# Self-attention of a decoder layer: where v's store to DRAM stands in the queue, and which queues begin v's four copies

## The chip, the cores and the metric

The kernel runs on one core of a Trainium2 chip. The metric is the device time of one launch in microseconds (us), as the median of three runs. Everything is 32-bit floating point. Besides the timed runs there is one execution recorded by the hardware profiler; its page and trace are what the text reads from.

## The reference

A decoder layer works on x of shape (2, 1024, 256): self-attention, cross-attention to a context of 77 rows, and a feed-forward part that only half of the tokens pass through, each followed by an addition and a layer norm. The change touches the self-attention only:

```python
q, k, v = split_heads(x @ Wq), split_heads(x @ Wk), split_heads(x @ Wv)   # 16 heads of 64
q, k = apply_rope(q), apply_rope(k)
sim = where(causal, einsum('bid,bjd->bij', q, k) * 64 ** -0.5, -inf)
out = einsum('bij,bjd->bid', softmax(sim, axis=-1), v)
x = layernorm(x + merge_heads(out) @ Wo + bo)
```

## The kernel before

**Pairs.** Two heads make a pair of 128 columns. There are 2 x 8 = 16 pairs, numbered 0 to 15, and an object `Pair` has one method for each step. Tokens are cut in eight tiles of 128. The steps have short names in lists of text: a number in front of a name is the pair's, and in the list `steps` the number beside a name says which pair is meant, relative to the period: `("w", 1)` in period 5 is for pair 6, `("V7", -1)` for pair 4. So three pairs are in work at once: in one period the outputs of pair n-1, the scores of pair n and the projections of pairs n+1 and n+2. The first two pairs follow a list of their own (`opening`), the last ones another (`ending`). The order of the instructions on each engine, and of the DMAs on each queue, is the order of these lists; each engine and each queue takes its own in that order, and an instruction that waits holds all behind it.

**The steps that matter here**, with their lines:

- `P` and `E`: projections on TensorE (L268 for q and k, L303 for v) and their evacuation by ScalarE (L276 into `raw`, L312 into `v`). `Ek1` fills the second half of `raw`, `Ev4` and `Ev0` fill the two halves of `v`. The tile `v` has one buffer: pair n+2's `Ev0` may write it only after pair n+1's `v` has been stored.
- `d0`, `d1` (`swap`, L219): two DMAs each, from SBUF to SBUF, that swap neighbouring partitions of `raw` into `turned`, for tokens 0 to 511 and for tokens 512 to 1023. `c`, `s`, `a`: GpSimd's multiplications by cosine (L288), by sine (L291) and the addition (L295) that make the rotated k and q.
- `S0` to `S4`: scores on TensorE (L342). `S0` needs only the first half of the rotated k and q, `S1` is the first that needs the second half.
- `T`, `X`, `R`: masked minimum on VectorE (L355), exponentials on ScalarE (L363), transposes on VectorE (L372).
- `w` (`spread`, through `begin`, L219): one DMA on SP's queue that stores `v`, 512 KB, into a DRAM tile `v_d`.
- `l` (`copies`, L322): four DMAs that load `v_d` into `v4` four times, each into other 32 partitions, 512 KB each. They stand on the queue of ScalarE, which begins them between its own instructions. The tile `v4` has one buffer, so they wait for the outputs of the pair before.
- `V0` to `V7` (`output`, L410): the products of the probabilities with `v4`, 488 small matmuls a pair, 64 columns by 32 rows, with a weight load for each. `S0` stands before `V0`, `S1` between `V1` and `V2`, `S2` between `V4` and `V5`, `S3` behind `V7`.
- `O`: evacuation of the outputs (L422). `D` and `B` (L219): the inverse sums go to DRAM (`inv_d`) and come back spread over 128 partitions (`over`). `M` multiplies on GpSimd, `W` stores the pair's output.

**The gate.** `begin` puts a DMA on SP's queue. The last matmul of `V1` is left in the list `gate`; the next DMA that goes through `begin` takes it out and waits for that matmul. In the list `steps` the next one is `d0` of pair n+1, and so `d0`, `B`'s two DMAs and `w`'s one follow one another on SP's queue once `V1` is done.

Of the kernel before, what the change touches and what calls it, by code (L numbers as in the profile page):

```python
# [17 lines left out]
B, T, C = 2, 1024, 256  # L18
# [4 lines left out]
NT = T // P  # L23
# [11 lines left out]
def decoder_layer(  # L35
# [23 lines left out]
    nc = tc.nc  # L59
# [80 lines left out]
    keys = [(b, hp) for b in range(B) for hp in range(NP)]  # L140
# [5 lines left out]
    with (  # L146
# [99 lines left out]
        class Pair:  # L246
# [71 lines left out]
            def copies(self):  # L318

                self.v4 = s1.tile([P, K4, P], F32, tag="v4", name="v4")  # L320
                for r in range(4):
                    nc.scalar.dma_start(  # L322
                        self.v4[r * R32 : (r + 1) * R32, :, :].rearrange("k (c n) d -> k c (n d)", c=4),
                        self.v_d.rearrange("c k e -> k c e"),
                    )
# [73 lines left out]
            def output(self, n):  # L399
                if n == 0:  # L400
                    self.po = [ring.tile([P, NT, R32], F32, tag="t", name="po_self") for _ in range(4)]
                for k in range(4):
                    for j in range(2):
                        first = (NT * n + n, NT * (n + 1) + n)[j]
                        step = (1, NT)[j]
                        last = first + (NT - 1 - n) * step + 1

                        for r in range(k if n == NT - 1 else 0, 4):
                            rows = slice(r * R32, (r + 1) * R32)
                            ins = TE.matmul(  # L410
                                self.po[r][j * D : (j + 1) * D, n:, :],
                                self.v4[rows, NT * k + n, j * D : (j + 1) * D],
                                p_t[rows, first:last:step, k * R32 : (k + 1) * R32],
                                start=(n == 0 and k == 0), stop=(n == NT - 1 and k == r),
                            )
                if n == 1 and self.n < len(keys) - 1:
                    gate[:] = [ins]

            def gathered(self, r):
# [18 lines left out]
        class Closing:  # L438
# [47 lines left out]

        steps = [
# [40 lines left out]
            0Ev4 0T01 1Pq1 0X00 0c1 0s1 0X01 1Eq1 1Ek1 1Pv0 0a1 0S1 2L 0R00 0w 0R01 1d1 1Pv4 1c1 1Pq0 0T10 0T11  # L528
            0S2 1Ev4 0T21 0X10 1Ev0 1Eq0 1Pk0 1s1 1w 0X11 2Pq1 0T20 0l 0R10 1Ek0 1d0 0S3 0R11 0X21 0X20 0T30
            2Pk0 1a1 0T31 0X30 1c0 0S4 0X31 0R20 1s0 0R30 0R21 1a0 2Eq1 0T40 3L 2Pv4 0T41 2Pv0 0X40 0X41 2Ek0  # L530
            0R31 0R40 2Pq0 2Ev4 5= 1S0 0R41 1T00 2Eq0 2Ev0 0V0 1T01 0V1 2w 0V2 1S1 1T11 0V3 1X00 2d0 0V4 0V5 1T10
            1S2 1X01 1X11 1R00 0V6 0V7 1X10 0O0 1T20 1T21 1S3 1R10 1R01 0O1 2c0 1l 1X20 1T31 2Pk1 0O3 1T30 0O2
            3Pv4 0Q 2Ek1 1S4 2c1 1X30 2s0 1X21 3Pq1 1R20 3Ev4 3Pv0 2a0 1R11 3Pk0 0I 1T41 2d1 1R30 1X31 3Pq0 1T40
            2S0 1R21 1X41 1X40 1R31 1R40 0D 1R41 2T00 3Ek0 2s1 3Eq1 4L 2a1 3Eq0 3Ev0 1V0 1V1 0B 2T01 2X00 1V2 2S1
            1V3 1V4 2T10 2T11 1V5 2R00 2S2 2X01 2T20 2T21 1V6 2X11 2R01 1V7 3d0 3c0
        """


        ending = """
            14S3 14R11 15s0 14X20 12M 14R20 14X10 14X21 14R10 13O0 14l 13O1 14R21 14T31 15Pk1 15a0 13Q 14T30 13I  # L540
            14S4 14X31 14X30 13O2 14R31 14T41 14X41 14T40 14R30 14R41 4C 12W 13D 15Ek1 15d1 5A 15c1 4Y 13O3 14X40 14R40
            15S0 15s1 15T01 15a1 14V0 15T00 15X01 14V1 13B 14V2 15S1 14V3 14V4 15T10 15T11 15X00 14V5
            15R00 15X11 15S2 14V6 14V7 15X10 15T20 15T21 14O0 15R01 15S3 14O3 5C 15R10 15l 15X21 13M 15T30 15X20
# [602 lines left out]
```

## Time and profile before

| | us |
|---|---|
| median of 3 runs | 831.27 (830.59 to 837.27) |
| profiled execution, its own time | 842.25 |
| its span | 840.5 |
| TensorE busy in the span | 796.4 (95%) |
| VectorE, ScalarE, GpSimd busy | 581.4, 356.6, 367.6 |
| outputs (L410), first to last matmul | 57.3 to 553.6 |

A time of the profiled execution is counted from the start of its span; 1.75 us of its own time lie outside. It took 11 us more than the median of the timed runs. "x" in front of a number counts instructions. A time in square brackets in the timeline is how long the engine stood idle before the row, and what ended the wait; "issue" stands for idle time in which the engine waited for nothing that the profile shows. The mean granted TensorE clock was 0.985 of the full one. Queue q1 holds the DMAs that SP began, q10 those of ScalarE, and q8 brings TensorE's instructions: 90 packets, 1.47 MB, so 16 KB each.

### The profile page before, as it was taken

The numbers are of one execution on the slowest core, as the hardware profiler recorded it, in microseconds if no ns is written. First come the engines' busy times: TensorE is split into PE (matmuls) and PEld (weight loads), VectorE is DVE, ScalarE is ACT, GpSimd is POOL, SyncE is SP. The second block draws the span as 40 slices with busy tenths as digits, with TensorE's granted clock in tenths as the row PEclk, the third lists the DMA queues.
The fourth block names the chain that finished last, engine by engine and source line by source line (L and its number), as shares of the span: only waits on it lengthen the run. The fifth ranks groups of instructions, "written<-read, shape, count | busy, mean of one in ns | idle before, by whom it ended". The sixth has DMA issues, their size and how long they took to land.

```text
span 840.5 us, 26580 instructions
## 1 busy us (share of the span) xinstructions
PE 796.4 (95%) x11432; PEld 629.2 (75%) x11432; DVE 581.4 (69%) x1345; ACT 356.6 (42%) x842; POOL 367.6 (44%) x261
## 2 busy tenths in 40 slices
PE   8999999999999899999999989899999999998996
PEld 4566688888788787788787867589778888876655
DVE  2558679668668568668776796535477788876673
ACT  2545455556456455554544554200443332333220
POOL 2733554555454554463661653213032222261574
PEclk9999999999999999999999999899999999999999
DMA  5445387577468467567474585564360000011131
GB/s 176 140 135 138 117 216 181 180 197 195 128 168 205 149 187 184 172 170 183 161 195 130 150 208 161 130 188 151 132 210 1 1 1 0 1 51 51 51 101 50
DMA packets 65328, 112.32 MB, mean 134 GB/s; under 512 B 6497, under 2 KB 43707, under 8 KB 65211
## 3 DMA queue, kind: packets, MB, share of 16 engines
q1 hardware_dynamic: 54459, 72.87, 26.9%
q10 hardware_dynamic: 9216, 33.56, 18.6%
q0 software_dynamic: 1536, 4.20, 1.3%
q8 instruction: 90, 1.47, 0.8%
q14 instruction: 27, 0.22, 0.1%
HBM read 71.24 MB, written 22.59 MB: 112 GB/s over the span
## 4 chain that ended last, share of the span: by engine, by line
PE 79%; DVE 10%; issue 4%; POOL 4%; DMA 1%; ACT 1%; POOLq 0%; SPq 0%; DVEq 0%; ACTq 0%
PE po_self L410 17%; PE ps_scores L342 16%; PE pp_kq L268 13%; PE pp_v L303 7%; PE po_proj L473 5%; PE ps_cross L945 5%; PE po_cross L997 4%; DVE reach L800 2%; PE pp_h L888 2%; PE po_ffn L899 2%; DVE pT L372 2%; PE unread L244 1%; PE pt_p L977 1%; POOL e L966 1%; POOL comp L830 1%
## 5 line engine op out<-in xcount | busy, mean ns | idle before, releaser
L355 DVE CUSTOM_DVE_ANT_0 p<-ps_scores,fence 128x512 f32<-128x512 f32 (+7 forms) x256 | 179.7, 751 | 127.2 <-PE ps_scores L342 126.8
L363 ACT ACTIVATE p<-p,neg 128x768 f32<-128x768 f32 (+7 forms) x256 | 196.3, 768 | 162.5 <-DVE neg L355 160.6
L410 PE MATMUL po_self<-pT,v 32*64 32x256 f32 (+6 forms) x7808 | 160.4, 298 | 22.3 <-issue 17.5
L372 DVE STREAM_TRANSPOSE pT<-p 128x768 f32<-128x768 f32 (+7 forms) x256 | 175.8, 740 | 3.4 <-ACT p L363 1.8
L410 PEld LDWEIGHTS po_self<-pT,v 32*64 32x64 f32 x7808 | 139.1, 133 | 47.6 <-issue 36.3
L342 PE MATMUL ps_scores<-kq 64*128 64x256 f32 (+3 forms) x1056 | 151.8, 420 | 2.9 <-issue 1.3
L342 PEld LDWEIGHTS ps_scores<-kq 64*128 64x128 f32 x1056 | 95.0, 191 | 45.2 <-issue 29.8
L291 POOL TENSOR_TENSOR turned<-turned,sin 128x1024 f32<-128x1024 f32 x31 | 73.1, 2360 | 109.7 <-DMA turned<-raw 105.0
L268 PE MATMUL pp_kq<-xT,w_pair 128*128 128x256 f32 (+2 forms) x516 | 118.8, 382 | 1.3 <-ACT xT L203 0.8
L288 POOL TENSOR_TENSOR kq<-raw,cos 128x1024 f32<-128x1024 f32 x31 | 73.3, 2363 | 103.8 <-ACT raw L276 103.8
L268 PEld LDWEIGHTS pp_kq<-xT,w_pair 128*128 128x128 f32 x516 | 87.1, 191 | 25.2 <-issue 11.3
L966 POOL TENSOR_TENSOR e<-e,inv 128x616 f32<-128x616 f32 x32 | 38.2, 1215 | 113.8 <-DVE inv L965 96.1
L120 POOL TENSOR_TENSOR rs<-ve,neg_half 128x1 f32<-128x1 f32 x48 | 27.6, 577 | 113.3 <-DVE ve L118 112.1
L295 POOL TENSOR_TENSOR kq<-kq,turned 128x1024 f32<-128x1024 f32 x31 | 73.4, 2369 | 1.4
L997 PE MATMUL po_cross<-packed,pT 128*128 128x256 f32 (+1 forms) x320 | 72.5, 381 | 0.0
L945 PE MATMUL ps_cross<-wqk,x1T 128*128 128x308 f32 x256 | 69.2, 423 | 0.0
L997 PEld LDWEIGHTS po_cross<-packed,pT 128*128 128x128 f32 (+1 forms) x320 | 60.7, 192 | 8.9
L303 PEld LDWEIGHTS pp_v<-w_pair,xT 128*128 128x128 f32 x512 | 61.1, 192 | 4.0 <-issue 2.2
L303 PE MATMUL pp_v<-w_pair,xT 128*128 128x128 f32 x512 | 62.2, 275 | 0.0
L945 PEld LDWEIGHTS ps_cross<-wqk,x1T 128*128 128x128 f32 x256 | 47.4, 190 | 16.2 <-issue 0.7
L958 ACT ACTIVATE e<-e 128x616 f32<-128x616 f32 x32 | 22.9, 717 | 83.0 <-DVE e L954 83.0
L473 PE MATMUL po_proj<-wo,attnT 128*128 128x256 f32 x224 | 51.6, 381 | 1.5 <-ACT out_pair L422 1.0
(128 smaller groups left out, 830.7 us busy)
## 6 DMA issues: line engine op xcount, KB each, us to landing
v<-v_d ACTq DMA_DIRECT2D x64, 512.0 KB, 8.4
turned<-raw SPq DMA_DIRECT2D x64, 256.0 KB, 4.5
v_d<-v SPq DMA_DIRECT2D x16, 512.0 KB, 4.6
over<-inv_d SPq DMA_DIRECT2D x32, 256.0 KB, 4.7
attn_d<-out_pair SPq DMA_DIRECT2D x14, 512.0 KB, 3.8
attnT<-attn_d SPq DMA_DIRECT2D x8, 512.0 KB, 5.4
vo_d<-vo SPq DMA_DIRECT2D x2, 1232.0 KB
attnT<-attn_d SPq DMA_DIRECT2D x3, 768.0 KB, 6.5
```

The source lines that it names most:

```text
L268: TE.matmul(pp[:, cols], self.w[:, c, "kq".index(of), :], x_ts[self.b, n][:, c, cols], start=(c == 0), stop=(c == NC - 1),)
L288: E.tensor_tensor(self.kq[:, :, n * NB : (n + 1) * NB], self.raw[n], self.twice(cos, n), ALU.mult)
L295: E.tensor_tensor(dst, dst, self.turned[n], ALU.add)
L303: TE.matmul(pv[:, i, :], x_ts[self.b, 2 * n // NT][:, c, toks], self.w[:, c, 2, :], start=(c == 0), stop=(c == NC - 1),)
L342: TE.matmul(self.ps[j][:, cols], self.kq[rows, 1, t * P : (t + 1) * P], self.kq[rows, 0, cols.start - at : cols.stop - at], start=True, st ...
L355: V.tensor_tensor_reduce(p[:, span], self.ps[j][:, span], fence[:, T - (t + 1) * P :], -SCALE, -MASKED, ALU.add, ALU.min, neg[:, i : i + 1],)
L363: A.activation(p[:, span], p[:, span], AF.Exp, bias=neg[:, i : i + 1], scale=-1.0, accum_out=self.sums[:, j, t : t + 1],)
L372: V.transpose(p_t[:, first : first + t * step + 1 : step, :], self.p[g, j][:, span].rearrange("p (n k) -> p n k", k=P),)
L410: ins = TE.matmul(self.po[r][j * D : (j + 1) * D, n:, :], self.v4[rows, NT * k + n, j * D : (j + 1) * D], p_t[rows, first:last:step, k * R ...
L473: TE.matmul(self.po, of, wo[:, c, :], start=(c == 0), stop=(c == NP - 1))
L945: TE.matmul(ps[:, g, : Q * S], self.x_t[:, c, :], wqk[:, c, self.b, h : h + Q, :].rearrange("p h s -> p (h s)"), start=(c == 0), stop=(c = ...
L997: TE.matmul(po, self.p_t[:w, k, :], packed[self.b][:w, k, :], start=(k == 0), stop=(k == NK - 1))
```

## The change

There are three edits:

1. `w` moves from behind `V1` (after `d0` and `B`) to behind `V7` of the same period, and the last matmul of `V7` is left in `gate` too, so that the store waits for it. In the ending, `15w` is put at the front for the same reason. SP's order in a period was: `d0` (2 DMAs), `B` (2), `w` (1), `d1` (2), and so on. It becomes: `d0` (2), `B` (2), `w` (1, now waiting for `V7`), two of `l`'s copies, `d1` (2), and so on.
2. In the opening, `2d0` moves ahead, so that it and not `2w` is what takes `V1`'s gate, and `3d0` moves ahead of `0B` for the same reason.
3. Of `l`'s four copies the first and third stay on ScalarE's queue, and the second and fourth go to SP's.

The instructions of TensorE, VectorE and GpSimd are the same and in the same order, and so are the computing ones of ScalarE.

```diff
                 for r in range(4):
-                    nc.scalar.dma_start(
+                    (nc.scalar, nc.sync)[r % 2].dma_start(
                         self.v4[r * R32 : (r + 1) * R32, :, :].rearrange("k (c n) d -> k c (n d)", c=4),
                         self.v_d.rearrange("c k e -> k c e"),
                     )
...
-                if n == 1 and self.n < len(keys) - 1:
+                if n in (1, NT - 1) and self.n < len(keys) - 1:
                     gate[:] = [ins]
...
-            ("T00", 0), ("T01", 0), ("s1", 0), ("V0", -1), ("a1", 0), ("V1", -1), ("d0", 1), ("B", -2), ("w", 1), ("S1", 0), ("V2", -1),
+            ("T00", 0), ("T01", 0), ("s1", 0), ("V0", -1), ("a1", 0), ("V1", -1), ("d0", 1), ("B", -2), ("S1", 0), ("V2", -1),
...
-            ("V6", -1), ("T21", 0), ("V7", -1), ("X10", 0), ("X20", 0), ("O1", -1), ("S3", 0),
+            ("V6", -1), ("T21", 0), ("V7", -1), ("w", 1), ("X10", 0), ("X20", 0), ("O1", -1), ("S3", 0),
...
-            ... 0V0 1T01 0V1 2w 0V2 1S1 1T11 0V3 1X00 2d0 0V4 0V5 1T10
-            1S2 1X01 1X11 1R00 0V6 0V7 1X10 ...
+            ... 0V0 1T01 0V1 2d0 0V2 1S1 1T11 0V3 1X00 0V4 0V5 1T10
+            1S2 1X01 1X11 1R00 0V6 0V7 2w 1X10 ...
...
-            ... 1V0 1V1 0B 2T01 2X00 1V2 2S1
-            1V3 1V4 ... 1V7 3d0 3c0
+            ... 1V0 1V1 3d0 0B 2T01 2X00 1V2 2S1
+            1V3 1V4 ... 1V7 3c0
...
-            14S3 14R11 15s0 ...
+            15w 14S3 14R11 15s0 ...
```

More of the change, by code (lines that the diff above doesn't have):

```diff
@@ L530, in decoder_layer @@
             2Pk0 1a1 0T31 0X30 1c0 0S4 0X31 0R20 1s0 0R30 0R21 1a0 2Eq1 0T40 3L 2Pv4 0T41 2Pv0 0X40 0X41 2Ek0
-            0R31 0R40 2Pq0 2Ev4 5= 1S0 0R41 1T00 2Eq0 2Ev0 0V0 1T01 0V1 2w 0V2 1S1 1T11 0V3 1X00 2d0 0V4 0V5 1T10
-            1S2 1X01 1X11 1R00 0V6 0V7 1X10 0O0 1T20 1T21 1S3 1R10 1R01 0O1 2c0 1l 1X20 1T31 2Pk1 0O3 1T30 0O2
+            0R31 0R40 2Pq0 2Ev4 5= 1S0 0R41 1T00 2Eq0 2Ev0 0V0 1T01 0V1 2d0 0V2 1S1 1T11 0V3 1X00 0V4 0V5 1T10
+            1S2 1X01 1X11 1R00 0V6 0V7 2w 1X10 0O0 1T20 1T21 1S3 1R10 1R01 0O1 2c0 1l 1X20 1T31 2Pk1 0O3 1T30 0O2
             3Pv4 0Q 2Ek1 1S4 2c1 1X30 2s0 1X21 3Pq1 1R20 3Ev4 3Pv0 2a0 1R11 3Pk0 0I 1T41 2d1 1R30 1X31 3Pq0 1T40
-            2S0 1R21 1X41 1X40 1R31 1R40 0D 1R41 2T00 3Ek0 2s1 3Eq1 4L 2a1 3Eq0 3Ev0 1V0 1V1 0B 2T01 2X00 1V2 2S1
-            1V3 1V4 2T10 2T11 1V5 2R00 2S2 2X01 2T20 2T21 1V6 2X11 2R01 1V7 3d0 3c0
+            2S0 1R21 1X41 1X40 1R31 1R40 0D 1R41 2T00 3Ek0 2s1 3Eq1 4L 2a1 3Eq0 3Ev0 1V0 1V1 3d0 0B 2T01 2X00 1V2 2S1
+            1V3 1V4 2T10 2T11 1V5 2R00 2S2 2X01 2T20 2T21 1V6 2X11 2R01 1V7 3c0
         """
         ending = """
-            14S3 14R11 15s0 14X20 12M 14R20 14X10 14X21 14R10 13O0 14l 13O1 14R21 14T31 15Pk1 15a0 13Q 14T30 13I
+            15w 14S3 14R11 15s0 14X20 12M 14R20 14X10 14X21 14R10 13O0 14l 13O1 14R21 14T31 15Pk1 15a0 13Q 14T30 13I
             14S4 14X31 14X30 13O2 14R31 14T41 14X41 14T40 14R30 14R41 4C 12W 13D 15Ek1 15d1 5A 15c1 4Y 13O3 14X40 14R40
```

## The prediction

> **What bounds the kernel now.** I read the page first, then the list of waits, and then the timeline of TensorE and of the DMA queues around one pair.
>
> ```profile
> PE 796.4 (95%) x11432; PEld 629.2 (75%) x11432; DVE 581.4 (69%) x1345; ACT 356.6 (42%) x842; POOL 367.6 (44%) x261
> ...
> q8 instruction: 90, 1.47, 0.8%
> ...
> PE po_self L410 <- issue: 17.5, 16, 2.4
> ```
>
> TensorE is busy for 95% of the span, so while the pairs run only what it waits for can be won. The third row (waits: us in total, times, longest) says what that is in the output products: 17.5 us in 16 stalls in which nothing visible is missing. The second row gives a suspect, TensorE's own instructions: 90 packets of 16 KB. An output matmul with its weight load takes 2 of 256 places in such a packet and 18 ns or so (3.5 us for 128), so in `V2` to `V7` TensorE eats one packet in 2.4 us.
>
> The timeline of TensorE and SP for one pair (start, us, row):
>
> ```profile
> 280.18 3.86 PE L410 MATMUL po_self<-pT,v 32*64 32x192 f32 x192
> 283.96 1.56 PE L342 MATMUL ps_scores<-kq 64*128 64x512 f32 x8
> 285.45 1.05 PE L410 MATMUL po_self<-pT,v 32*64 32x96 f32 x65
> 288.86 1.43 PE L410 MATMUL po_self<-pT,v 32*64 32x64 f32 x103 [2.36 <-issue]
> ...
> 278.53 1.11 SPq L219 DMA_DIRECT2D turned<-raw  x2
> 279.69 2.87 SPq L219 DMA_DIRECT2D over<-inv_d  x2
> 282.65 0.54 SPq L219 DMA_DIRECT2D v_d<-v  x1
> ```
>
> and the queues in the stretch from 286.2 to 288 (packets, MB, share):
>
> ```profile
> q1 hardware_dynamic: 18, 0.04, 5.3%
> q8 instruction: 1, 0.02, 3.6%
> ```
>
> The stall always stands some 103 matmuls before the pair's end, a fixed place in the program, as the end of an instruction packet would be. The trace's packets, one by one, say why: q8's packet began at 286.40, when v's store was just ending (its last packet began before 286.6), took 1.04 us, and TensorE went on 1.4 us later. In all eleven pairs listed below the same 1.2 to 1.5 us lie between the end of that packet and the end of the stall. In the pair that stalled least of those with the same place (0.64 us, ending at 488.53) the packet got in front of the store's: it began 9.4 us after `V0`, where in this pair it was 11.6.
>
> **Edit 1, gain.** The store leaves the stretch between `V1` and `V7`. The timeline's stalls of this kind end at 132.67, 192.72, 224.25, 257.14, 288.86, 321.69, 352.07, 385.88, 419.49, 453.96 and 488.53: 1.46 + 0.44 + 1.60 + 1.32 + 2.36 + 2.09 + 0.97 + 1.19 + 0.77 + 1.98 + 0.64 = 14.8 us; one in pair 1 (1.28 us, before scores at 101.66) has a store beside it as well. That is 16.1 us in 12 stalls. The other two L410 stalls in the opening (0.79 and 0.89) come when q1 is quiet and stay. What is left of each: `over`'s packets end 9.3 to 10.2 us after `V0`, so the instruction packet can begin at about 9.4 to 10; with 1.0 us for itself and 1.4 until it is used, 0 to 0.7 us of stall stays. I take 0.35 for each: 16.1 - 12 x 0.35 = **11.9 us gained**. Ends: 16.1 (nothing left), and 16.1 - 12 x 0.64 = 8.4 (all become like the best).
>
> Two rules of the Trainium skill speak against it. "Runtime: NRT & Kernel Launch" (Instruction fetch mechanics) calls the cost of crossing a 16 KiB block mostly hidden: by it the edit brings 0. "DMA: Bandwidth & Descriptors" (Queues, rings and completion order) says that an SDMA engine changes between queue rows after each packet: the fetch would then wait for one of the store's packets, 0.17 us by the trace, and 12 x 0.17 = 2 us could be won. The rows say otherwise: 14.8 us of stalls, and a fetch that starts when the store ends. I go by the rows, and keep the rules' 0 to 2 us as a rival.
>
> **Edit 1, cost.** The store's 512 KB (1.9 us of packets) now move behind `V7`, where 2 MB of copies move already. Who is behind it: on SP's queue two copies, then `d1`. The copies are not urgent for `V0`: they end some 12 us after `V7`, and `V0` comes 16 us or more after it. `d1` is. In pair 6's period (ScalarE's copies begin at 258.69):
>
> ```profile
> 264.22 1.13 SPq L219 DMA_DIRECT2D turned<-raw  x2
> ...
> q10 hardware_dynamic: 238, 0.84, 102.7%
> ...
> turned<-raw SPq DMA_DIRECT2D x2, 256.0 KB, 8.1
> ...
> 273.01 2.35 POOL L291 TENSOR_TENSOR turned<-turned,sin 128x1024 f32<-128x1024 f32 x1 [4.08 <-DMA turned<-raw]
> 275.44 2.39 POOL L295 TENSOR_TENSOR kq<-kq,turned 128x1024 f32<-128x1024 f32 x1
> ...
> 278.25 2.00 PE L342 MATMUL ps_scores<-kq 64*128 64x512 f32 x12
> ```
>
> The second and third rows are the queues between 264 and 268: `d1` is begun, but only q10 moves anything, and `d1` lands 8.1 us after its issue instead of 4.5 (the page's median). So one queue's DMAs stand behind the other's. From there sine and addition end at 277.83, and `S1` (last row) starts at 278.25: 0.42 us to spare. In the same way the tight pairs 2, 3, 4, 6 and 8 have 0.26, 0.60, 1.01, 0.42 and 0.59 us, 0.58 on average; pair 1 has 0.85, pair 0 1.5, pairs 5 and 7 2.4, pairs 9 to 12 about 4. `V7`, `d1` and `S1` all move with TensorE, so only a delay relative to `V7` counts. If `d1` comes x us later, TensorE loses 5 (x - 0.58) and what the next ones add.
>
> **Edit 3** decides x. "DMA: Bandwidth & Descriptors" (Issuing engines are not separate DMA queues) says that starting DMAs from two engines saves only the sequencer's time. By it the order stays one line, 512 KB + 2 MB, and x = 1.9: a loss of 5 x 1.32 + 1.05 + 0.4 = 8.1 us, and 3.8 remain of the gain. The trace bears the rule out for `d1` behind copies, but has another row: the windows give the copies 201, 205 and 199 GB/s at a DMA share of 1.0, while 296 GB/s follow where `d1` joins (270 to 272). So the copies' packets are slow in themselves and room is left. A copy fills 32 partitions only. The trace shows no copies on two queues; the bounds are +1.9 (one line) and about -2.5 (store beside the first copy, second beside third: four steps of 2.5 us become three). I take x = 1.0, nearer to the row of `d1`: 5 x 0.42 + 0.15 = **2.3 us lost**.
>
> **The rest at nothing.** ScalarE issues two DMAs less a pair (about 0.45 us each; its `O2` waited 1.37 us behind them in pair 6): it isn't what TensorE waits for. `Ev0` must not overwrite `v` before the store has landed: pair 6's `V7` ended at 258.4 and `Ev0` ran at 264.11, 5.7 us later; the store took 4.6 from issue to landing. About 1 us of cover, and beyond it ScalarE has waits of 1 to 2 us for VectorE. Edit 2: `2d0` was begun 0.4 us behind `2w` before, `3d0` 1.2 us behind `0B`: nothing, as GpSimd takes them later. The ending: the last pair's copies no longer wait in ScalarE's queue (they took 3.8 us to begin at 519.4, and `V0` waited 1.60 us for them at 535.44), but on SP they hold back pair 13's output store and the load behind it, begun at 515.18 and 515.55, by about 5 us, before a projection at 527.55. Gain of 1.6, loss of 2: taken as 0.
>
> **Sum.** -11.9 + 2.3 = -9.6 us against the profiled execution's own time: 842.25 becomes 832.7. The median is 11 us below that execution. If those 11 us were stalls like these, few would be left in the timed runs; I take nine tenths of the gain: 831.27 - 8.8 = **822.5 us**.
>
> **Rivals.** *One line* (20%): v's store and the copies keep one order as for `d1`, x = 1.9, gain 3.8: 827.5. For it: the 264 to 268 rows. Against: the copies leave half of the rate seen elsewhere unused. *The fetch is late anyway* (13%): `over` or `d0` hold it, or its own way is long, and only the 2 us of the packet rule are won: 829. For it: the opening's two stalls with a quiet q1. Against: the fetch's start follows the store's end. *Copies in each other's way* (15%, slower): first and second copy, on two queues, share whatever slows a copy, and the store is between them. `d1` is the place. At x = 2.4 the loss (9x - 10) equals the 11.9 gained, above it the kernel is slower; at x = 3.5 it is 21.5 - 11.9 = +9.6: 841. That `V7`'s gate doesn't take hold is no rival: the next DMA through `begin` behind `V7` is the store in every period.
>
> **The numbers.** Forecast 52%, from 814 (nothing left, x below 0.5) to 827. A measurement of this kernel can tell about 1% (8.3 us: 823.0) from no change. Of the forecast's 52% some 44 are faster than that, with 3 from the other cases: 47%. Within 1%: 8 from it, 30 from the rivals: 38%. Slower: 15%. The range runs from 814 to 834: it takes in both milder rivals and the near part of the slow one.
>
> **What would show it.** Right: L410's "issue" falls from 17.5 us to 4 to 7; in the SP rows `v_d<-v` starts just behind each pair's last L410; `S1` shows no wait for L295 or at most 1 us in the tight pairs; q10 and q1 both move packets behind `V7`. Wrong on the gain: the stalls before the last 103 matmuls stay at 1 us or more with the store gone. Wrong on the cost: scores waiting for GpSimd's L295 in pairs 2 to 8, or `d1`'s landing over 10 us.

## The result, and the profile after

The changed kernel takes 0.994 of the time of the kernel before, with a 95% interval from 0.9921 to 0.9959: 0.6% faster. On that chip the medians are 831.32 us (20 runs, 826.07 to 835.54) and 837.5 us (20 runs of the kernel before, 830.59 to 844.79). The profiled execution after took 831.2 us, its span 829.4, at a mean granted TensorE clock of 0.987. Before, the span was 840.5. So the forecast had the right sign, and it was too high: 822.5 to 831.27 would have been a ratio of 0.989. The difference that the runs show is inside the 1% that the prediction took as "no change that can be told".

The page after, its TensorE row and the queue of its instructions:

```profile
PE 791.2 (95%) x11432; PEld 626.6 (76%) x11432; DVE 584.4 (70%) x1345; ACT 356.0 (43%) x842; POOL 367.9 (44%) x261
...
q8 instruction: 90, 1.47, 0.8%
```

and two rows of its list of waits (us in total, times, longest):

```profile
PE po_self L410 <- issue: 8.4, 15, 1.1
PE po_proj L473 <- DMA attnT<-attn_d: 7.3, 1, 7.3
```

The first row is the gain: the output products' idle time without a visible reason was 17.5 us and is 8.4. The second row was not there before. It is one wait of 7.3 us, in the ending, and it is nearly as large as what the first row gives.

The timeline of TensorE and of SP for the pair that the prediction showed (start, us, row):

```profile
278.62 1.05 PE L410 MATMUL po_self<-pT,v 32*64 32x96 f32 x65
280.20 1.43 PE L410 MATMUL po_self<-pT,v 32*64 32x64 f32 x103 [0.53 <-issue]
...
271.93 1.11 SPq L219 DMA_DIRECT2D turned<-raw  x2
273.08 1.92 SPq L219 DMA_DIRECT2D over<-inv_d  x2
281.71 0.35 SPq L219 DMA_DIRECT2D v_d<-v  x1
282.10 1.31 SPq L322 DMA_DIRECT2D v<-v_d  x2
287.61 1.14 SPq L219 DMA_DIRECT2D turned<-raw  x2
```

The stall of 2.36 us is one of 0.53, at the same place of the program. SP now begins the store just behind the pair's last output product, then two copies, then `d1`.

Behind that `V7`, between 283 and 287.5, the two queues (packets, MB, share) and one copy's way from issue to landing:

```profile
q10 hardware_dynamic: 234, 0.89, 66.4%
q1 hardware_dynamic: 135, 0.49, 30.6%
...
v<-v_d SPq DMA_DIRECT2D x1, 512.0 KB, 11.8
```

Here both queues move at once, where in the prediction's stretch of four microseconds only q10 did. What `d1` makes of it, on GpSimd and then on TensorE, in pair 6's period:

```profile
266.42 2.36 POOL L291 TENSOR_TENSOR turned<-turned,sin 128x1024 f32<-128x1024 f32 x1 [4.09 <-DMA turned<-raw]
268.86 2.38 POOL L295 TENSOR_TENSOR kq<-kq,turned 128x1024 f32<-128x1024 f32 x1
...
271.64 2.00 PE L342 MATMUL ps_scores<-kq 64*128 64x512 f32 x12
```

The addition ends at 271.24 and `S1` starts at 271.64: 0.40 us to spare, where it was 0.42. `d1` is not late.

Last, the ending after, on SP and on TensorE:

```profile
504.48 1.49 SPq L322 DMA_DIRECT2D v<-v_d  x2
506.06 0.40 SPq L219 DMA_DIRECT2D attn_d<-out_pair  x1
506.51 11.69 SPq L219 DMA_DIRECT2D attnT<-attn_d  x2
...
506.08 3.72 PE L473 MATMUL po_proj<-wo,attnT 128*128 128x256 f32 x16
509.73 1.99 PE L342 MATMUL ps_scores<-kq 64*128 64x512 f32 x8
...
519.26 6.59 PE L473 MATMUL po_proj<-wo,attnT 128*128 128x256 f32 x16 [7.33 <-DMA attnT<-attn_d]
```

and the same store, load and projection before, with the first products of pair 15 behind them:

```profile
515.18 0.33 SPq L219 DMA_DIRECT2D attn_d<-out_pair  x1
515.55 3.61 SPq L219 DMA_DIRECT2D attnT<-attn_d  x2
...
527.55 3.72 PE L473 MATMUL po_proj<-wo,attnT 128*128 128x256 f32 x16 [0.96 <-ACT out_pair L422]
...
535.44 0.61 PE L410 MATMUL po_self<-pT,v 32*64 32x256 f32 x2 [1.60 <-DMA v<-v_d]
537.52 2.87 PE L410 MATMUL po_self<-pT,v 32*64 32x256 f32 x48 [1.47 <-DVE x L121]
```

The load's way from issue to landing (us, last number), before and after:

```profile
attnT<-attn_d SPq DMA_DIRECT2D x1, 512.0 KB, 5.6
...
attnT<-attn_d SPq DMA_DIRECT2D x1, 512.0 KB, 12.6
```

SP now begins two of the last pair's copies first, then pair 13's output store (`attn_d`), then the load `attnT` that the next projection reads. `V7` of pair 14 ends at 504.46, so this store is begun 1.6 us after it; before, it was begun 3.7 us ahead of that `V7`'s end at 518.9. And the load, which now moves together with 2 MB of copies, landed 12.6 us after its issue instead of 5.6. TensorE stands for 7.33 us. The projection behind the wait then takes 6.59 us for the 16 matmuls that took 3.72 in the row above it.

**Where the 11 us between the two spans come from.** At `V0` of pair 14 the changed kernel leads by 14.95 us (489.42 against 504.37). At `V0` of pair 15 it leads by 5.43 (527.60 against 533.03). At the end it leads by 11.1 again, as the kernel before has losses of its own in pair 15: its `V0` waited 1.60 us for the copies and 1.47 us for VectorE, and its outputs then ran for 6.8 us at a granted clock of 0.50. So the pairs gave about what was hoped for and more, and the ending took two thirds of it. These are two single executions: the medians of the timed runs differ by 6.2 us.

### The profile page after: what moved, and what is told of

Its sections match the earlier page's. It is cut to its first block, busy times and chain, and to the rows that moved or that the text cites. A ratio compares the mean times of both kernels' runs of the same rounds, so it can differ in the third digit from the quotient of the medians.

```text
span 829.4 us, 26596 instructions
## 1 busy us (share of the span) xinstructions
PE 791.2 (95%) x11432; PEld 626.6 (76%) x11432; DVE 584.4 (70%) x1345; ACT 356.0 (43%) x842; POOL 367.9 (44%) x261
## 3 DMA queue, kind: packets, MB, share of 16 engines
q8 instruction: 90, 1.47, 0.8%
## 4 chain that ended last, share of the span: by engine, by line
PE 80%; DVE 9%; POOL 3%; issue 3%; DMA 2%; ACT 1%; SPq 0%; POOLq 0%; DVEq 0%; ACTq 0%
PE po_self L410 17%; PE ps_scores L342 16%; PE pp_kq L268 14%; PE pp_v L303 7%; PE po_proj L473 6%; PE ps_cross L945 5%; PE po_cross L997 4%; DVE reach L800 2%; PE pp_h L888 2%; PE po_ffn L899 2%; POOL comp L830 2%; PE unread L244 2%; DMA attnT<-attn_d 2%; PE pt_p L977 1%; POOL e L966 1%
## 5 line engine op out<-in xcount | busy, mean ns | idle before, releaser
L410 PE MATMUL po_self<-pT,v 32*64 32x256 f32 (+6 forms) x7808 | 154.3, 294 | 10.0 <-issue 8.4
L410 PEld LDWEIGHTS po_self<-pT,v 32*64 32x64 f32 x7808 | 136.3, 130 | 32.0 <-issue 24.4
L295 POOL TENSOR_TENSOR kq<-kq,turned 128x1024 f32<-128x1024 f32 x31 | 73.5, 2370 | 1.4
L473 PE MATMUL po_proj<-wo,attnT 128*128 128x256 f32 x224 | 54.5, 397 | 8.4 <-DMA attnT<-attn_d 7.3
```

What stands on the lines that cost most here:

```text
L295: E.tensor_tensor(dst, dst, self.turned[n], ALU.add)
L410: ins = TE.matmul(self.po[r][j * D : (j + 1) * D, n:, :], self.v4[rows, NT * k + n, j * D : (j + 1) * D], p_t[rows, first:last:step, k * R ...
L473: TE.matmul(self.po, of, wo[:, c, :], start=(c == 0), stop=(c == NP - 1))
```

## The experiments

Theory A: the change does in the pairs what the prediction says; what is missing was lost in the ending, where pair 13's store and load stand behind the last pair's copies and behind `V7`'s gate. Rival B: the gain is small because the fetch of the instructions is late for other reasons. Rival C: v's copies on two queues get in each other's way.

### The changed kernel again (e0_after, f0_after)

No edit. The experiments stand in three groups, each on a chip of its own: e0 to e3, e4 to e7, f0 to f3. Times are compared inside a group.

> The changed kernel once more, as the mark for the others on the same chip. Theory (ending): 0.993 to 0.996 of the kernel before, about 5 us faster, as in the 20 runs. In the profile: L410's issue stalls near 8 us, and one wait of 5 to 8 us of a projection (L473) for the load of attnT in the ending.

> The changed kernel once more, beside the version with the mended ending, so that the two are compared on the same chip. Both theories: 0.990 to 0.995 of the kernel before; L410's issue 8 to 11 us; the last pairs' projection (L473) waits 6 to 8 us for attnT.

Measured: 0.9917 (0.9892 to 0.9941; 831.81 us against 837.93) and 0.9946 (0.992 to 0.9972; 828.65 against 834.23). L473's wait for `attnT` is 6.7 and 7.1 us, L410's issue 10.7 and 4.7. So the wait of some 7 us belongs to this kernel, while the stalls differ from execution to execution.

### The load first (e1_load_first)

```diff
-            ... 5C 15R10 15l 15X21 13M 15T30 15X20
+            ... 5C 15R10 13M 13W 6A 15l 15X21 15T30 15X20
```

> The changed kernel, but in the ending pair 13's output store and the load behind it (13M 13W 6A) stand ahead of the last pair's copies (15l) in the list, so that on SP's queue they go first. Theory (ending): the pairs win about 10 us, and 4 to 6 us of it are given back in the ending because that load stands behind two copies that wait for V7; here they are kept: 826 or so, 0.987 to 0.990 of before, 4 to 6 us below the changed kernel; the 7.3 us wait of L473 for attnT is gone or under 1 us. Rival (traced only): timed runs stall less than the profiled one, so the pairs win only 5 us there and the last pair's outputs wait for VectorE's transposes anyway: within 1.5 us of the changed kernel.

Measured: 0.9906 (0.9872 to 0.9941), 829.83 us; the gain of 4 to 6 us on the changed kernel (0.9917) did not come. SP in the ending, and the projection:

```profile
505.50 0.35 SPq L219 DMA_DIRECT2D attn_d<-out_pair  x1
505.89 1.12 SPq L219 DMA_DIRECT2D attnT<-attn_d  x1
507.06 1.51 SPq L322 DMA_DIRECT2D v<-v_d  x2
...
516.63 5.38 PE L473 MATMUL po_proj<-wo,attnT 128*128 128x256 f32 x16 [3.44 <-DMA attnT<-attn_d]
```

Store and load are ahead of SP's copies now, the load lands in 10.6 us, and half of the wait is left. The store is still begun at the very end of `V7` (505.4): with no `w` behind pair 14's `V7`, the next DMA that passes `begin` is this store, and it takes the gate. So two things hold the load back, and the order of the list is only one of them.

### All copies on ScalarE's queue again (e2_copies_act)

```diff
-                    (nc.scalar, nc.sync)[r % 2].dma_start(
+                    nc.scalar.dma_start(
```

> The changed kernel with edit 3 undone: all four copies on ScalarE's queue, the store still behind V7. Theory (ending, with the copies' order): the swap d1 comes about 1.9 us later after V7 than before, since store and copies stand in one line, so S1 waits for GpSimd's addition (L295) by 1 to 1.5 us in pairs 2, 3, 4, 6 and 8, a loss of about 7 us; but the ending's load is in time again, a gain of 5: about the changed kernel's time, within 3 us. Rival (store costs nothing behind V7): no S1 wait appears, and it is 4 to 6 us faster than the changed kernel through the ending alone.

Measured: 0.9908 (0.987 to 0.9946), 832.1 us, not to be told from the changed kernel on the same chip (0.9917). Three rows of its waits and its SP row in the ending:

```profile
PE po_proj L473 <- DMA attnT<-attn_d: 7.7, 1, 7.7
PEld ps_scores L342 <- POOL kq L295: 3.8, 6, 1.2
PE ps_scores L342 <- POOL kq L295: 1.4, 3, 0.8
```

```profile
506.75 0.33 SPq L219 DMA_DIRECT2D attn_d<-out_pair  x1
```

No copy stands on SP's queue, and still the store starts only when `V7` ends (506.7): here the gate alone holds it back. The load then takes 14.9 us to land, beside four copies on ScalarE's queue, so it is slow beside copies even where none is ahead of it on its own queue. The other two rows show what edit 3 spares: scores wait for L295, though less than the 7 us expected. From `V7`'s last matmul to GpSimd's sine behind `d1`, the mean over the five tight pairs 2, 3, 4, 6 and 8 is 14.69 us in the kernel before; with the store behind `V7` and one queue it is 15.30 here and 15.29 in e5_act_no_gate; with two queues it is 14.44, 14.59, 14.42, 14.56, 14.78 and 14.31 in the changed kernel, e0, f0, e1, e4 and f1, a mean of 14.52. So x, the delay of `d1`, is +0.6 us on one queue and -0.2 on two, where single executions lie between -0.4 and +0.1.

### Two queues alone (e3_two_queues)

The kernel before, with edit 3 and nothing else.

> The kernel before with edit 3 alone: second and fourth copy on SP's queue, the store still behind V1. Theory (ending): L410's issue stalls stay at 15 to 18 us, copies end earlier, and the ending's load is late: 3 to 6 us slower than before, 1.003 to 1.007. Rival (the gain comes from the two queues): as fast as the changed kernel, 0.993 to 0.996.

Measured: 0.5% slower, 1.0049 (1.0017 to 1.008), 841.77 us. L410's issue is 18.1 us, as before. The ending, SP and TensorE:

```profile
519.26 1.30 SPq L322 DMA_DIRECT2D v<-v_d  x2
520.66 0.40 SPq L219 DMA_DIRECT2D attn_d<-out_pair  x1
...
534.05 6.65 PE L473 MATMUL po_proj<-wo,attnT 128*128 128x256 f32 x16 [7.06 <-DMA attnT<-attn_d]
```

`V7` has no gate here. The store is late because SP has two copies ahead of it that wait for `V7`. So each of the two edits is enough for a wait of this size (7.7 us in e2, 7.1 here), and a kernel with both has two reasons for it. That fits e1, which took away one and kept 3.4 us of wait. Why e1, with the gate left, waits less than e2 is not shown apart; its load landed sooner, 10.6 us against 14.9. Rival C falls with e2 and e3: putting the copies on one queue brings no gain, and a wait as long as e3's whole loss stands in the ending.

### The ending mended (e4_ending, f1_ending)

The order of e1, and no gate behind the `V7` of pair 14, which has no store of v to hold:

```diff
-                if n in (1, NT - 1) and self.n < len(keys) - 1:
+                if n in (1, NT - 1) and self.n < len(keys) - (1 if n == 1 else 2):
```

> The first experiment's order in the ending (13M 13W 6A ahead of 15l) and, with it, no gate left by pair 14's V7, which has no store behind it and so catches pair 13's output store (13W). Theory (gate in the ending): that store and the load behind it are begun when GpSimd has multiplied, some 3 us before V7's end, as in the kernel before; the wait of L473 for attnT, 6.7 us in the changed kernel and 3.4 in the first experiment, is under 0.5 us, and the time is 4 to 6 us below the changed kernel: 0.985 to 0.988 of before. Rival (VectorE's chain sets the last pair's outputs): the wait goes, but V0 of pair 15 then waits for transposes or for v4, and it gains under 2 us on the first experiment.

> The version with the mended ending (pair 13's store and load ahead of pair 14's copies, and no gate behind pair 14's V7) once more. Theory (the ending ate what was missing of the gain): 5 to 8 us below the changed kernel in the same rounds, that is 0.983 to 0.989 of the kernel before, no attnT wait at L473. Rival (the ending's wait only moves to pair 15's copies and tails): within 2 us of the changed kernel.

Measured: 0.9866 (0.9823 to 0.9909), 824.88 us against 836.93, and in the third group 0.9864 (0.9811 to 0.9917), 820.48 us against 834.23. The changed kernel in that third group is at 828.65, so the ending is worth 8.2 us there by the medians, and 6.8 by the two ratios. SP and TensorE in the ending of f1:

```profile
497.15 0.34 SPq L219 DMA_DIRECT2D attn_d<-out_pair  x1
497.54 0.44 SPq L219 DMA_DIRECT2D attnT<-attn_d  x1
501.38 1.59 SPq L322 DMA_DIRECT2D v<-v_d  x2
...
508.66 3.62 PE L473 MATMUL po_proj<-wo,attnT 128*128 128x256 f32 x16
...
516.73 6.07 PE L410 MATMUL po_self<-pT,v 32*64 32x256 f32 x262 [1.05 <-DVE inv L384]
```

The store is begun during `V7`, the load lands in 5.4 us, and L473 waits for nothing and takes 3.62 us instead of 6.59. Behind it `V0` of pair 15 waits 1.05 us for VectorE. Theory A holds, and this version is faster than both kernels.

### The mended ending with all copies on ScalarE (e5_act_no_gate)

e2 with the gate of e4.

> The changed kernel with edit 3 undone (all copies on ScalarE's queue) and no gate left by pair 14's V7. Theory (gate in the ending): L473's wait for attnT falls from 7.7 us to under 1 us with nothing else changed, 4 to 6 us less than with edit 3 undone alone; the waits of S1 for L295, some 5 us, stay, so 827 to 829. Rival (copies in front of the load): the wait stays at 5 us or more.

Measured: 0.9896 (0.9871 to 0.9921), 826.49 us, beside 0.9866 for e4 in the same group. The `attnT` wait is gone here too, with the old order of the list: without copies on SP's queue, the gate was the only thing in the way. Whether edit 3 adds anything to the time stays open, as the intervals of e4 and e5 overlap.

### v stored twice (e7_store_twice)

The kernel before, with a second store of v, into a DRAM tile that nothing reads, right behind the first: twice the suspected cost.

```diff
+                twin = dram.tile([4, R32, NT * P], F32, tag="twin", name="twin_d")
+                begin(twin.rearrange("r k e -> (r k) e"), self.v.rearrange("p n d -> p (n d)"))
```

> The kernel before with v stored twice behind V1, the second time into DRAM that nobody reads: the suspected cost doubled in its place. Theory (the store holds the instruction packet back): the packet comes up to 2 us later still, L410's issue grows from 17.5 us to 30 or more, and the time by 12 to 25 us, 1.015 to 1.03. Rival (an engine changes between queues after each packet): one more 4 KB packet at most, and the time is within 3 us of before.

Measured: 1.2% slower, 1.0116 (1.0042 to 1.019); the median of its four runs is 846.68 us. From its waits:

```profile
PE po_self L412 <- issue: 24.0, 17, 2.7
```

17.5 us became 24.0 (the line is L412 here), and the stalls before the last 100 to 107 products, summed over pairs 1 to 12, are 19.7 us against 15.5 before and 4.6 after; in e3, where one store stands behind `V1` again, they are 14.8. The store makes most of the stalls: without it they shrink, with two they grow. Rival B falls. But they did not double, and both expectations missed the size. The packets of q8 say why: the fetch in question begins, as a mean over these pairs, 9.4 us after `V0` with no store beside it, 10.5 with one and 10.8 with two (at most 9.9, 11.6 and 12.2). The last packets of the stores began 10.9 to 12.5 us after `V0` with one and 11.9 to 14.1 with two. So the second store mostly moves when the fetch already got through, and a fetch does not always wait for a store's end: in pair 11 of the kernel before it began 1.9 us ahead of the store's last packet.

### The sums' broadcast earlier (e6_over_early, f2_over_early)

e4, with `over`'s two DMAs begun ahead of `V0` instead of behind `d0`: is what is left of the stalls theirs?

```diff
-            ... ("a0", 0), ("R40", -1), ... ("d0", 1), ("B", -2), ("S1", 0),
+            ... ("a0", 0), ("B", -2), ("R40", -1), ... ("d0", 1), ("S1", 0),
```

> The kernel with the mended ending, and B (over, 512 KB) ahead of V0 instead of behind V1, so that only d0 moves between V1 and V7. Theory (any bulk DMA there holds the fetch): the 0.2 to 0.9 us that stay of each stall are over's, they go to 0.3 or less, L410's issue falls from 10 us to 5 or 6, and the time by 3 to 4 us. Rival (the fetch's own way): the rest of the stalls is what a fetch takes with quiet queues; L410's issue stays at 9 to 10 us and the time too, or it grows where over delays an earlier packet.

> The same with over's two broadcasts begun ahead of V0 instead of behind d0. Theory (the instruction packet's own way now sets the stall, what is left is 0.5 us a pair): the stalls 100 to 107 output products before a pair's end stay near 5 us in sum over pairs 1 to 12, and the time is within 1.5 us of the version with the mended ending. Rival (over's packets hold the third instruction packet): the sum falls below 2 us, and the time is 3 to 5 us lower.

Measured: 0.9874 (0.9832 to 0.9917), 825.41 us, and 0.9885 (0.9829 to 0.9941), 823.85 us: no faster than e4 and f1. The stalls at the known place do go, to 1.1 and 0.5 us in sum over pairs 1 to 12 (e4 6.2, f1 2.5). But L410's issue in total is 10.8 and 10.6 us, against 9.0 and 5.8:

```profile
PE po_self L410 <- issue: 10.6, 12, 2.7
```

The stalls moved. In e6 one of 1.12 us stands in `V4` of pair 6, where an earlier packet is due, and in f2 seven of 0.5 to 1.5 us stand at that place. So `over`'s packets do hold back the third instruction packet, and begun elsewhere they hold back another one, as the last clause of e6's rival had it. The expectation of f2 that the packet's own way sets what is left was wrong. The longest stall of both runs, 2.7 us, stands in pair 15, where e4 and f1 have 1.1; the list of the ending is the same in all four, and the cause of this one stays open.

### d0 put back in the opening (f3_d0_back)

f1 without edit 2: `2d0` behind `1X00`, `3d0` behind `1V7`.

> The mended ending with the opening's d0 put back (2d0 behind 1X00, 3d0 behind 1V7; v's store stays behind V7). Theory (edit 2 is worth nothing, as the prediction has it): within 1.5 us of the version with the mended ending. Rival (the early swap is worth something in the opening): 2 to 4 us above it, with GpSimd's L291 or S1 of pairs 2 and 3 waiting for turned<-raw.

Measured: 0.9906 (0.9874 to 0.9938), 826.03 us, 5.5 above f1 in the same group. SP, GpSimd and TensorE in the opening:

```profile
100.18 1.13 SPq L219 DMA_DIRECT2D turned<-raw  x2
...
110.78 2.35 POOL L291 TENSOR_TENSOR turned<-turned,sin 128x1024 f32<-128x1024 f32 x1 [18.44 <-DMA turned<-raw]
...
120.21 1.22 PE L342 MATMUL ps_scores<-kq 64*128 64x256 f32 x4 [5.35 <-POOL kq L295]
```

`3d0` is now the first DMA behind `1V7`, takes its gate and starts at 100.18; with edit 2 (f1) it starts at 92.45. GpSimd waits 18.44 us for it and TensorE 5.35. Both the expected time and the rival's were too low. In the kernel before, `3d0` was begun at 93.95 and no scores of pairs 2 and 3 waited long for it (0.33 us at most), so there edit 2 had nothing to win; no run has edit 2 alone. Without it, edit 1 would have cost these 5.4 us.

## Why the prediction was wrong

- **The ending: "Gain of 1.6, loss of 2: taken as 0".** This is the step that failed. The prediction saw that SP's copies would hold pair 13's store and load back by about 5 us, and they did (5.3 us relative to `V7`). It left out two terms. The load behind the store would then run beside 2 MB of copies: 12.6 us to landing instead of 5.6, which alone is 7.0 us. And a pause of 7.3 us costs more than itself: the 16 matmuls behind it, at half the clock, took 6.59 us instead of 3.72, 2.9 us more. In sum TensorE lost 7.3 + 2.9 = 10.2 us at a place that cost 0.96 us before. In the timed runs the mended ending is worth 7 to 8 us (f1 against f0).
- **"That `V7`'s gate doesn't take hold is no rival: the next DMA through `begin` behind `V7` is the store in every period."** True in the periods, wrong behind pair 14's `V7`: there is no pair 16, so no store of v follows, and the gate fell on pair 13's output store. With edit 3 undone the gate alone was enough for a wait of 7.7 us (e2), and without it that wait was gone (e5). The ending is a list of its own and had to be walked through DMA by DMA, as the periods were.
- **Edit 1, gain: 11.9 us.** Nearly right in size, and right that the store delays the fetch; "a fetch that starts when the store ends" holds in some pairs only. In pairs 1, 2, 5, 7, 8 and 12 of the kernel before it starts within 0.6 us of the store's last packet, in pairs 6, 11 and 13 it starts 1.9 to 2.7 us ahead of it, and there TensorE stalled too. At the same places 5.1 us of stalls are left in pairs 1 to 13 (0.92, 0.49, 0.51, 0.47, 0.53, 0.17, 0.23, 0.40, 0.88 and 0.49) of 16.1, so 11.0 are saved. "0.35 for each" of 12 was 4.2; it is 5.1. Other executions of the changed kernel have 5.1 (e0) and 2.6 (f0), and e3, with the store behind `V1`, 16.6. L410's issue did not fall to "4 to 7" but to 8.4, since the stalls of the opening and the ending stayed and one of 0.31 us came in pair 12.
- **The two rules against it.** The Trainium skill's rule that crossing a block is mostly hidden ("Runtime: NRT & Kernel Launch", Instruction fetch mechanics) gave 0, and the profile was nearer. The 2 us were a misreading: the skill's round robin ("DMA: Bandwidth & Descriptors", Queues, rings and completion order) goes by packets of typically 9 to 17 descriptors, and the prediction took one 4 KB packet of the trace for such a packet. The store is 128 of those, 8 for each of 16 engines if evenly spread; if each is a descriptor, all 8 may be one packet of the rule, 8 x 0.17 = 1.4 us (an estimate). The fetch came 1.2 us later with the store than without (10.54 against 9.37 us after `V0`, as means), so the rule need not speak against the stalls; which it is, no run here shows.
- **A gain that was not in the sum.** The lead of 14.95 us at `V0` of pair 14 is more than 11.0. The clock accounts for most of the rest, by an estimate. In the kernel before, three of the stalls (pairs 5, 7 and 12) are followed by a stretch of 3.4 us at half clock; if TensorE is busy all through it, it loses half of each, 1.7 us: 5.1 us. The changed kernel has one such stretch in the pairs (behind pair 1's stall): 1.7. That is 3.4 us; with the 11.0, 14.4 of 14.95. e0 and f0 have no such stretch in the pairs, e3 four and e7 five.
- **Edit 1, cost, and edit 3: x = 1.0, 2.3 us lost.** Mis-sized, on the careful side: x was -0.2 (14.52 against 14.69), and scores wait for L295 only 0.6 us in sum. The prediction read the Trainium skill ("DMA: Bandwidth & Descriptors", Issuing engines are not separate DMA queues) as one line in a fixed order, in which the store delays `d1` by its own 1.9 us; the section says that the DMAs interleave on the same 16 engines, and gives no order. The runs have +0.6 with one queue and -0.2 with two. So the trace's other row, the rate that a copy leaves unused, was the better guide.
- **Edit 2 at nothing.** The traces fit it for the kernel before; but beside edit 1 it was not free to leave out (f3, 5.5 us).
- **Nine tenths, and the base.** The sum for the profiled execution was -9.6 us, and it came to -11.1 (842.25 to 831.2), by other parts than thought: 11.0 + 3.4 gained in the pairs, 0 instead of 2.3 lost at `d1`, and the ending. That the two sums lie so close is luck. Nine tenths of 9.6 is 8.6 and not 8.8, which moves the forecast by 0.2 us. The three timed runs before had a median of 831.27; of 20 runs on that chip it is 837.5, and single runs of one kernel spread over 14 us. So the base itself was some 6 us low by chance, and the 11 us between it and the profiled execution were not a sign that few stalls are left in the timed runs.
- **The rivals.** None of the three is what happened. "One line" fits the time best (a ratio of 0.995), but by coincidence: its mark, scores waiting for L295, is missing (0.6 us in sum).

## What to carry to other kernels

When a store is moved in a list that repeats, walk through the list's two ends as well: name, for the last round, which transfer takes the wait that the store used to take, and what stands behind it on that queue. When a large transfer begins earlier or on another queue, size the small, urgent loads beside it by what they take in its company, not alone. A wait of a few microseconds on TensorE is to be charged with the slower clock behind it, and a stall that is taken away may give that back as well.

## What the runs showed of the hardware

**The clock follows even short pauses.** Windows of the kernel before around pair 5's stall of 1.60 us (the columns are stretch, length, busy time and number of each engine, granted clock, DMA share, GB/s):

```profile
216.60:222.60 6.00, 6.00 (x269) 4.95 (x268) 5.77 (x17) 2.93 (x8) 2.49 (x2) 1.00 0.72 227
224.30:225.60 1.30, 1.30 (x103) 1.26 (x102) 1.30 (x4) 0.17 (x1) 0.50 (x1) 0.99 0.07 13
225.60:229.00 3.40, 3.40 (x18) 2.65 (x18) 0.36 (x2) 1.12 (x4) 0.00 (x0) 0.50 0.61 160
```

and of the changed kernel behind the wait of 7.3 us:

```profile
519.20:523.00 3.80, 3.74 (x9) 3.03 (x10) 0.00 (x0) 0.00 (x0) 0.00 (x0) 0.50 0.59 198
```

The clock is full until the stall, and 1.3 us after its end it is 0.50 for 3.4 us. The Trainium skill ("TensorE: Matmul & The Clock Gate", What's actually happening) has the gate drop to one half after an idle window of about 3.4 us and open again after a busy one, with windows that run on freely. The factor and the length agree with these rows. The pause doesn't: stalls of 1.60, 2.36, 1.98 and once 0.92 us were enough, while others of 2.09 and 1.46 us had no such stretch behind them. Part of that is where a stall falls. The stretches of the kernel before begin at 225.58, 290.44, 454.27 and 536.20, whole multiples of 3.413 us apart (19, 48 and 24), as windows on a fixed grid would. On this grid the stall of 2.09 us falls into two windows, with 1.55 and 0.54 us. How much of a window must be idle, these runs don't tell: in the kept traces, from 88 to 545 us, every window with 1.8 us or more idle was followed by half clock, and of those with 0.9 to 1.8 us some were and some not.

**A fetch of 16 KB of instructions comes later beside a store of 512 KB.** Doubling the store raised these stalls from 15.5 to 19.7 us over twelve pairs, and removing it left 4.6; the fetch began 9.4, 10.5 and 10.8 us after `V0` with none, one and two stores. **A load of 512 KB that landed in 5.4 to 5.6 us ahead of most of the copies took 10.6 to 14.9 us together with them** (e1 10.6, the changed kernel 12.6, e2 14.9), and a copy on SP's queue took 11.0 us (median of the page) where one on ScalarE's took 7.4 in the same kernel, and 8.4 before.
